# Moving the stages of a local transformer's feed-forward: moments, norm and all behind them one place on

## The chip, the cores and the metric

The kernel runs on one core of a Trainium2 chip. The core's engines work side by side, each through its own queue in program order: TensorE (PE, matmuls and transposes, writing to PSUM), VectorE (DVE), ScalarE (ACT), GpSimd (POOL) and SyncE (SP), whose queue issues the DMAs. The metric is the device time of one execution in microseconds (us), shown as the median of several runs.

## The reference

The model is four layers, each a cross-attention and a feed-forward of its own kind, over x of shape (4, 512, 128). The change is in the third layer's feed-forward, a small transformer of six layers with local attention (windows of 32) and a gated feed-forward. Cut to what matters:

```python
def ffn_layer(x, g, bln, W1, b1, W2, b2):
    mu = x.mean(-1, keepdims=True)
    var = ((x - mu) ** 2).mean(-1, keepdims=True)
    xn = (x - mu) / jnp.sqrt(var + 1e-05) * g + bln
    hg = xn @ W1 + b1                       # 128 -> 2 * 341
    a, gate = jnp.split(hg, 2, -1)
    return a * jax.nn.gelu(gate, approximate=False) @ W2 + b2   # 341 -> 128
for i in range(DEPTH):                      # 6
    x = attn_layer(shift_tokens(x), Wqkv[i], q_scale[i], k_scale[i], Wo[i]) + x
    x = ffn_layer(shift_tokens(x), ln_g[i], ln_b[i], W1[i], b1[i], W2[i], b2[i]) + x
```

attn_layer has 16 heads of 64: queries and keys are normalised to length 1, scaled and rotated, then each window of 32 attends to itself and the window before it.

## The kernel before

The four layers follow one another. All but the local transformer are scheduled by a small planner (class Plan). The local transformer (local_transformer, L1690) is written out by hand: a Python loop emits the instructions in the order in which each engine's queue will run them, and waits come only from data and buffers.

The state Y[b] holds one batch's 512 tokens, features on partitions. A tile is 128 tokens of one batch in one layer: 6 x 4 x 4 = 96 tiles. A row is one batch in one layer, that is 4 tiles: 24 rows. The loop at L2028 runs over periods n and is a software pipeline: period n works on three tiles at once, T = tiles[n] (products with the query, key and value weights, rotation), T1 = tiles[n-1] (transposes, scores, softmax) and T2 = tiles[n-2] (probabilities, averages, output projection, residual). Since the last tile of row m finishes its residual in period 4m + 5, the feed-forward of row m starts in period 4m + 6. Its phase in a period is (n - 6) % 4.

The order within one period, shortened, with the two or three places of the feed-forward:

- queries_or_keys(T, 0, 0), probabilities(T2), queries_or_keys(T, 0, 1), rotate(T, 0, 0)
- **place 0** of the feed-forward (L2053)
- average(T2, 0), turned(T1, 0), queries_or_keys(T, 1, 0), normalised(T2, 0), rotate(T, 0, 1), and the same with the second half
- attended(T2), for a batch's last tile swap (a copy of Y for the next row's values), scores(T1), the last rotations, normalise(T), softmax(T1), project_out(T2), residual(T2)
- **place 2** (L2090: the norm, in phase 0)
- values(T, 0), values(T, 1)
- **place 1** (L2095)

The feed-forward's pieces and their engines: four PE transposes of Y and a ScalarE copy to xn (L1951, L1953); moments, eight small DVE instructions and two of POOL (L510 to L515); the norm, four of DVE (L522); the turn, four PE transposes and one ScalarE instruction (L1962, L1964); ff_gate, PE products and ScalarE's gelu (L1973, L1976); ff_up, PE products and a DVE product with the gate (L1984, L1987); ff_down, six PE instructions and an addition to Y in two halves on DVE (L1996, L1711). Chunks 0 and 1 of the 341 hidden features are full (128), chunk 2 has 85. In the kernel before, four phases hold them:

| phase | place 0 | place 2 | place 1 |
|---|---|---|---|
| 0 | transposes, copy, moments | norm | |
| 1 | turn | | gate 0, 1 |
| 2 | gate 2 | | up 0, 1 |
| 3 | up 2 | | down |

Buffers that matter: PSUM has the pair "sc" (two banks, one buffer), which the feed-forward's transposes and products, and the scores of T1, all take in turn; the next user waits until the last has been read. "av" is another single pair, for averages and the output projection. "mm" has two buffers, for the query and key products; "tr" has two, for transposes and values. In SBUF the rotation's second term "rs" has two buffers and is freed by POOL's sum (L1797). Weights of a layer are loaded by load(i) in period 16(i - 1) + 7, into buffers of the layer before the last one; the scaled rotation tables of the next layer are made on POOL (L1755, L1761) in periods with n % 16 == 15.

Of the kernel before, what the change touches and what calls it, by code (L numbers as in the profile page):

```python
# [238 lines left out]
def tile_kernel(ctx: ExitStack, tc: tile.TileContext, A: dict, out: bass.AP):  # L239
# [129 lines left out]
    with banks(), tc.tile_pool(name="prep", bufs=1) as prep:  # L369
# [3 lines left out]
        rows = prep.tile([8, D], F32, name="rows0")  # L373
# [94 lines left out]
    def col(r):  # L468
        return cols[:, r : r + 1]
# [35 lines left out]
    def moments(src):  # L505

        st = small.tile([128, NT, 6], F32, name="ln_st")
        mv = small.tile([128, NT, 2], F32, name="ln_mv")
        for t in range(NT):
            V.bn_stats(st[:, t], src[:, t])  # L510
        for t in range(NT):
            V.bn_aggr(mv[:, t], st[:, t])
        rs = small.tile([128, NT], F32, name="ln_rs")
        G.tensor_scalar(rs, mv[:, :, 1], 1e-5, None, ALU.add)
        G.tensor_tensor(rs, rs, mhalf[:, :NT], ALU.pow)  # L515
        return mv, rs

    def layernorm(dst, src, found=None):

        mv, rs = found or moments(src)  # L520
        for t in range(NT):
            V.tensor_scalar(  # L522
                dst[:, t], src[:, t], mv[:, t, 0:1], rs[:, t : t + 1], ALU.subtract, ALU.mult
            )
# [1165 lines left out]
    def local_transformer(Y):  # L1690
        with ExitStack() as es:
# [8 lines left out]
            def pair(tag):  # L1700

                t = homes["pair"].tile([128, 2, 512], F32, tag=tag, bufs=1, name=f"ps_{tag}")
                return t

            def add_y(b, t, bias=None):
                for r, o in ((slice(0, 64), 0), (slice(64, 128), 1)):
                    dst = Y[b][r, o : o + S]
                    if bias is None:
                        V.tensor_tensor(dst, t[r], dst, ALU.add)
                    else:  # L1710
                        V.scalar_tensor_tensor(dst, t[r], bias[r], dst, ALU.add, ALU.add)  # L1711
# [189 lines left out]
            def probabilities(T):  # L1901
                T.PT = tp.tile([128, LH // 2, 128], F32, name="PT", bufs=1)
                for g in range(2):
                    SC.copy(T.PT[:, 4 * g : 4 * g + 4], to_features(T.P[:, 4 * g : 4 * g + 4]))
# [40 lines left out]
                    V.tensor_tensor(dst, t[r], dst, ALU.add)  # L1945


            def ff_moments(F):
                F.t = pair("sc")[:, 0].rearrange("p (a b) -> p a b", b=128)
                for tt in range(NT):  # L1950
                    PE.transpose(F.t[:, tt], Y[F.b][:, 128 * tt : 128 * tt + 128], ident)  # L1951
                F.xn = lnp.tile([128, NT, D], F32, name="xn")
                SC.copy(F.xn, F.t)  # L1953
                F.found = moments(F.xn)

            def ff_norm(F):
                layernorm(F.xn, F.xn, F.found)

            def ff_turn(F):
                t = pair("sc")[:, 0]  # L1960
                for tt in range(NT):
                    PE.transpose(t[:, 128 * tt : 128 * tt + 128], F.xn[:, tt], ident)  # L1962
                F.xnT = lnp.tile([128, S], F32, name="xnT")
                SC.activation(  # L1964
                    F.xnT, t, AF.Identity, scale=col(R_LG + F.i), bias=col(R_LB + F.i)
                )
                F.h = tp.tile([128, 3, S], F32, name="fh", bufs=1)

            def ff_gate(F, *chunks):
                t = pair("sc")  # L1970
                for j, c in enumerate(chunks):
                    n, o = CH_W[c], DI + 128 * c
                    PE.matmul(t[:n, j], F.w1[:, o : o + n], F.xnT, start=True, stop=True)  # L1973
                for j, c in enumerate(chunks):
                    n = CH_W[c]
                    SC.activation(  # L1976
                        F.h[:n, c], t[:n, j], AF.Gelu, bias=col(R_B1 + (3 + c) * DEPTH + F.i)[:n]
                    )

            def ff_up(F, *chunks):  # L1980
                t = pair("sc")
                for j, c in enumerate(chunks):
                    n, o = CH_W[c], 128 * c
                    PE.matmul(t[:n, j], F.w1[:, o : o + n], F.xnT, start=True, stop=True)  # L1984
                for j, c in enumerate(chunks):
                    n = CH_W[c]
                    V.scalar_tensor_tensor(  # L1987
                        F.h[:n, c], t[:n, j], col(R_B1 + c * DEPTH + F.i)[:n], F.h[:n, c],
                        ALU.add, ALU.mult,
                    )  # L1990

            def ff_down(F):
                t = pair("sc")[:, 0]
                for c in range(3):
                    n = CH_W[c]
                    PE.matmul(t, F.w2[:n, c], F.h[:n, c], start=(c == 0), stop=(c == 2))  # L1996
                add_y(F.b, t, col(R_B2 + F.i))
# [7 lines left out]
                )  # L2005
                swapped[b] = t

            def ff_stage(F, phase, second):
                F.w1, F.w2 = loaded[F.i][3:5]
                if phase == 0 and not second:  # L2010
                    ff_moments(F)
                elif phase == 1:
                    ff_gate(F, 0, 1) if second else ff_turn(F)
                elif phase == 2 and second:
                    ff_up(F, 0, 1)
                elif phase == 2:
                    ff_gate(F, 2)
                elif phase == 3:
                    ff_down(F) if second else ff_up(F, 2)

# [1 line left out]
            rows = [Tile(i, b, 0) for i in range(DEPTH) for b in range(B)]  # L2024
            loaded = {0: load(0)}
            tabs = {0: tables(loaded[0][5])}
            swap(0)
            for n in range(len(tiles) + 10):  # L2028
                T = tiles[n] if n < len(tiles) else None
                T1 = tiles[n - 1] if 0 <= n - 1 < len(tiles) else None  # L2030
                T2 = tiles[n - 2] if 0 <= n - 2 < len(tiles) else None
                m, phase = divmod(n - 6, 4)
                F = rows[m] if 0 <= m < len(rows) else None
                if T:
                    if n % 16 == 7 and T.i + 1 < DEPTH:
                        loaded[T.i + 1] = load(T.i + 1)
                    if n == 4:
                        fill, send, send_back = clear(lnp, 1)
                        fill(G)
                        send(DMA)  # L2040
                        send_back(DMA)
                    if n % 16 == 15 and T.i + 1 < DEPTH:
                        tabs[T.i + 1] = tables(loaded[T.i + 1][5])
                    T.before = tiles[n - 1] if T.tt else None
                    T.w, T.wv, T.wo = loaded[T.i][:3]
                    T.tabs = tabs[T.i]
                    queries_or_keys(T, 0, 0)
                if T2:
                    probabilities(T2)
                if T:  # L2050
                    queries_or_keys(T, 0, 1)
                    rotate(T, 0, 0)
                if F:  # L2053
                    ff_stage(F, phase, False)
                if T2:
                    average(T2, 0)
                if T1:
                    turned(T1, 0)
                if T:
                    queries_or_keys(T, 1, 0)  # L2060
                if T2:
                    normalised(T2, 0)
                if T:
                    rotate(T, 0, 1)
                if T2:
                    average(T2, 1)
                if T1:
                    turned(T1, 1)
                if T:
                    queries_or_keys(T, 1, 1)  # L2070
                if T2:
                    normalised(T2, 1)
                if T:
                    rotate(T, 1, 0)
                if T2:
                    attended(T2)
                if T and T.tt == NT - 1 and n + 1 < len(tiles):
                    swap(tiles[n + 1].b)
                if T1:
                    scores(T1)  # L2080
                if T:
                    rotate(T, 1, 1)
                if T:
                    normalise(T)
                if T1:
                    softmax(T1)
                if T2:
                    project_out(T2)
                    residual(T2)
                if F and phase == 0:  # L2090
                    ff_norm(F)
                if T:
                    values(T, 0)
                    values(T, 1)
                if F:  # L2095
                    ff_stage(F, phase, True)

            for b in range(B):
                for r, o in ((slice(0, 64), 0), (slice(64, 128), 1)):
# [39 lines left out]
```

## Time and profile before

| what | value |
|---|---|
| median of 5 runs | 2558.78 us |
| lowest, highest | 2552.48, 2562.35 us |
| profiled execution | 2560.74 us |
| its span, first to last instruction | 2559.0 us |
| mean granted clock of TensorE | 0.944 |
| PE, DVE, ACT, POOL busy | 2290.8, 1789.6, 1243.1, 1540.0 us |
| first and last row maximum of the loop (L1893) | 579.9 and 2222.3 us |
| first and last instruction of the feed-forward's moments (L510) | 655.1 and 2242.1 us |

A line of the timeline gives start and duration in us, the engine, the source line, the operation, the tile written and those read with their shapes, and how many instructions of this kind stand together; behind it in brackets the idle time of that engine just before and what ended it. A line of the groups gives the count, the busy time in us, the mean in ns of one instruction, and the idle time before these instructions with what ended most of it. A busy PE is not PE at its peak: matmuls are pipelined and their ends are modelled.

### The profile page before, as it was taken

To read this page: it belongs to the slowest core of one execution; us is meant where nothing else is said; L and a number is where in the kernel's file an instruction comes from. 1 tells how busy PE (TensorE), PEld (TensorE's weight loads), DVE (VectorE), ACT (ScalarE), POOL (GpSimd) and SP (SyncE) were. 2 spreads that over 40 slices of the span, in tenths; PEclk is the share of its full clock that TensorE was granted. 3 is DMA by queue.
4 is the path that set the end of the run, shared out by engine and by line. 5 is a ranking of instruction groups with operands and counts; after the bars stand their busy time and mean duration, and the time that the engine had idled before them with its cause. 6 is when DMAs were issued, how large, how long until landed. Compare 5 with 4: busy or idle time off the path is not lost.

```text
span 2559.0 us, 87683 instructions
## 1 busy us (share of the span) xinstructions
PE 2290.8 (90%) x37341; PEld 1487.5 (58%) x37341; DVE 1789.6 (70%) x4016; ACT 1243.1 (49%) x2185; POOL 1540.0 (60%) x2613
## 2 busy tenths in 40 slices
PE   7968869968899999999999999999999999878676
PEld 3537624446666666666666666666666666634364
DVE  5533375758787888888888888788888888655422
ACT  3522225535555555555555555555555555423232
POOL 2332311348778777777777777877777777532333
PEclk9959969979999999999999999999999999978688
DMA  6210110014511112111211121111211111111022
GB/s 164 76 31 28 33 46 2 1 47 83 127 34 31 29 47 61 27 34 34 68 34 34 30 75 34 27 33 41 64 30 34 33 27 34 28 48 37 19 72 82
DMA packets 134305, 116.21 MB, mean 45 GB/s; under 512 B 29505, under 2 KB 102700, under 8 KB 133916
## 3 DMA queue, kind: packets, MB, share of 16 engines
q1 hardware_dynamic: 128373, 102.81, 15.4%
q0 software_dynamic: 4608, 7.35, 0.9%
q8 instruction: 296, 4.85, 0.8%
q14 instruction: 93, 0.76, 0.1%
q10 hardware_dynamic: 935, 0.43, 0.1%
HBM read 42.84 MB, written 21.52 MB: 25 GB/s over the span
## 4 chain that ended last, share of the span: by engine, by line
PE 57%; DVE 21%; issue 7%; POOL 5%; ACT 5%; DMA 3%; SPq 1%; another core or an unknown queue 1%; POOLq 0%; ACTq 0%; DVEq 0%
PE ps_tr L582 8%; PE ps_mm L1774 8%; PE ps_av L1938 4%; PE ps_av L1914 4%; PE ps_tr L1853 3%; DVE rc L1784 3%; DVE rs L1787 3%; DVE ss L1796 3%; PE ps_sc L1883 3%; PE ps_sc L1984 3%; PE ps_sc L1996 3%; PE ps L773 2%; PE ps L1312 2%; DVE P L1894 2%; PE ps L782 2%
## 5 line engine op out<-in xcount | busy, mean ns | idle before, releaser
L1797 POOL TENSOR_TENSOR rc<-rc,rs 128x512 f32<-128x512 f32 x384 | 488.2, 1274 | 232.4 <-DVE rs L1787 186.1
L1774 PE MATMUL ps_mm<-wqk,y 128*128 128x512 f32 x768 | 396.9, 599 | 10.6 <-DVE rs L1787 7.4
L1818 POOL TENSOR_TENSOR rc<-rc,rn_y 128x512 f32<-128x512 f32 x384 | 388.3, 1042 | 7.5
L1784 DVE TENSOR_TENSOR rc<-ps_mm,tabs 128x512 f32<-128x512 f32 x384 | 262.0, 682 | 159.4 <-ACT sq L1776 144.4
L1899 ACT ACTIVATE P<-P 128x1024 f32<-128x1024 f32 x96 | 101.5, 1057 | 424.1 <-DVE P L1894 424.1
L1776 ACT ACTIVATE sq<-ps_mm 128x512 f32<-128x512 f32 x384 | 230.7, 601 | 151.4 <-PE ps_mm L1774 103.0
L1787 DVE TENSOR_TENSOR rs<-ps_mm,tabs 128x512 f32<-128x512 f32 x384 | 261.1, 680 | 5.6 <-POOL rc L1797 5.5
L1796 DVE TENSOR_REDUCE ss<-sq 128x8 f32<-128x512 f32 x384 | 259.1, 675 | 0.0
L582 PE MATMUL ps_tr<-cst,rc 128*128 128x128 f32 x1536 | 210.5, 280 | 6.0 <-POOL rc L1818 4.4
L1914 PEld LDWEIGHTS ps_av<-v,PT 64*32 64x32 f32 x12288 | 137.4, 105 | 126.0 <-PE ps_tr L582 54.9
L1938 PE MATMUL ps_av<-aT,wo 128*128 128x128 f32 x1536 | 200.2, 283 | 4.8 <-issue 4.5
L1938 PEld LDWEIGHTS ps_av<-aT,wo 128*128 128x128 f32 x1536 | 180.6, 192 | 15.1 <-issue 6.6
L582 PEld LDWEIGHTS ps_tr<-cst,rc 128*128 128x128 f32 x1536 | 165.2, 141 | 25.8 <-POOL rc L1818 5.5
L1883 PE MATMUL ps_sc<-kT,qT 64*32 64x64 f32 x12288 | 147.2, 225 | 34.3 <-issue 27.1
L1914 PE MATMUL ps_av<-v,PT 64*32 64x65 f32 x12288 | 168.3, 225 | 6.0 <-DVE attn L1924 5.7
L1017 POOL DMA_INDIRECT back<-ye,to x80 | 77.7, 971 | 158.0 <-DVE ye L1131 113.1
L1883 PEld LDWEIGHTS ps_sc<-kT,qT 64*32 64x32 f32 x12288 | 140.5, 105 | 45.1 <-issue 31.0
L1774 PEld LDWEIGHTS ps_mm<-wqk,y 128*128 128x128 f32 x768 | 124.6, 192 | 60.9 <-issue 45.5
L763 ACT ACTIVATE P<-ps,deltaT 77x512 f32<-77x512 f32 x192 | 115.3, 682 | 82.2 <-PE ps L757 70.7
L1830 ACT COPY kT<-ps_tr 128x512 f32<-128x512 f32 x192 | 103.1, 589 | 81.5 <-PE ps_tr L582 81.5
L1830 ACT COPY qT<-ps_tr 128x512 f32<-128x512 f32 x192 | 103.2, 589 | 75.4 <-PE ps_tr L582 72.8
L1924 DVE TENSOR_TENSOR attn<-ps_av,la_den 128x512 f32<-128x512 f32 x192 | 132.7, 691 | 6.6
(392 smaller groups left out, 4502.2 us busy)
## 6 DMA issues: line engine op xcount, KB each, us to landing
v<-v SPq DMA_DIRECT2D x432, 65.0 KB
v<-v SPq DMA_DIRECT2D x96, 195.0 KB
wqk<-in_L_ffn_Wqkv_dram SPq DMA_DIRECT2D x24, 256.0 KB
sent<-xn SPq DMA_DIRECT2D x2, 2210.0 KB
xe<-sent SPq DMA_DIRECT2D x16, 260.0 KB
back<-xn SPq DMA_DIRECT2D x2, 2048.0 KB
raw<-in_L_ffn_W_dram SPq DMA_DIRECT2D x8, 512.0 KB
yb<-back SPq DMA_DIRECT2D x16, 256.0 KB
```

The costliest lines, as they stand in the source:

```text
L582: PE.transpose(t[:, i], src[:, i], ident)
L1774: PE.matmul(t, lhs, T.w[2 * kind + c], start=True, stop=True)
L1776: SC.activation(sq, t, AF.Square)
L1784: V.tensor_tensor(a, t, bc(T.tabs[:, 2 * kind, tt], [128, 8, LD], 1), ALU.mult)
L1787: V.tensor_tensor(r.rearrange("p h (x d) -> p h x d", x=2), t.rearrange("p h (x d) -> p h x d", x=2)[:, :, ::-1], bc(T.tabs[:, 2 * kind + ...
L1796: V.tensor_reduce(T.ss[:, kind, 8 * c : 8 * c + 8], sq, AX.X, ALU.add)
L1797: G.tensor_tensor(a, a, r, ALU.add)
L1818: G.tensor_tensor(a, a, bc(y[:, o : o + 8], [128, 8, LD], 2), ALU.mult)
L1830: SC.copy(t[:, 4 * c : 4 * c + 4, lead:], to_features(T.rot[kind, c].rearrange("p (k x) d -> p k (x d)", x=2)),)
L1883: PE.matmul(T.banks[32 * w : 32 * w + 32, z, k], T.qT[r, k, 32 * w : 32 * w + 32], T.kT[r, k, 32 * w : 32 * w + 64], start=False, stop=Tru ...
L1914: PE.matmul(T.means[32 * w : 32 * w + 32, x0, k], T.PT[r, 4 * g + k, 32 * w : 32 * w + 32], (T.v1 if w % 2 else T.v2)[r, x0, 4 * g + k], s ...
L1938: PE.matmul(t, T.wo[:, c], T.aT[:, c], start=(c == 0), stop=(c == 7))
```

## The change

The feed-forward of a row is spread over five periods; the fifth is at the same time the first of the next row. Transposes and copy stay where they were. Moments go from place 0 to place 2 of phase 0, the norm from place 2 of phase 0 to place 2 of phase 1, and everything behind it one period on. Up 2 and down of row m - 1 now stand in phase 0 of row m, up 2 just ahead of row m's transposes at place 0, and down at place 1.

| phase | place 0 | place 2 | place 1 |
|---|---|---|---|
| 0 | up 2 of the last row, transposes, copy | moments | down of the last row |
| 1 | | norm | |
| 2 | turn | | gate 0, 1 |
| 3 | gate 2 | | up 0, 1 |

The instructions, their shapes and their number stay the same.

```diff
-            def ff_moments(F):
+            def ff_tokens(F):
                 F.t = pair("sc")[:, 0].rearrange("p (a b) -> p a b", b=128)
                 for tt in range(NT):
                     PE.transpose(F.t[:, tt], Y[F.b][:, 128 * tt : 128 * tt + 128], ident)
                 F.xn = lnp.tile([128, NT, D], F32, name="xn")
                 SC.copy(F.xn, F.t)
-                F.found = moments(F.xn)
...
-            def ff_stage(F, phase, second):
-                F.w1, F.w2 = loaded[F.i][3:5]
-                if phase == 0 and not second:
-                    ff_moments(F)
-                elif phase == 1:
-                    ff_gate(F, 0, 1) if second else ff_turn(F)
-                elif phase == 2 and second:
+            def row(m):
+                F = rows[m] if 0 <= m < len(rows) else None
+                if F:
+                    F.w1, F.w2 = loaded[F.i][3:5]
+                return F
+
+            def ff_stage(m, phase, place):
+                F, last = row(m), row(m - 1)
+                if last and phase == 0 and place == 0:
+                    ff_up(last, 2)
+                if last and phase == 0 and place == 1:
+                    ff_down(last)
+                at = 3 * phase + place
+                if F and at == 0:
+                    ff_tokens(F)
+                elif F and at == 2:
+                    F.found = moments(F.xn)
+                elif F and at == 5:
+                    ff_norm(F)
+                elif F and at == 6:
+                    ff_turn(F)
+                elif F and at == 7:
+                    ff_gate(F, 0, 1)
+                elif F and at == 9:
+                    ff_gate(F, 2)
+                elif F and at == 10:
                     ff_up(F, 0, 1)
-                elif phase == 2:
-                    ff_gate(F, 2)
-                elif phase == 3:
-                    ff_down(F) if second else ff_up(F, 2)
...
-                if F:
-                    ff_stage(F, phase, False)
+                ff_stage(m, phase, 0)
...
-                if F and phase == 0:
-                    ff_norm(F)
+                ff_stage(m, phase, 2)
                 if T:
                     values(T, 0)
                     values(T, 1)
-                if F:
-                    ff_stage(F, phase, True)
+                ff_stage(m, phase, 1)
```

More of the change, by code (lines that the diff above doesn't have):

```diff
@@ L2032, in local_transformer @@
                 m, phase = divmod(n - 6, 4)
-                F = rows[m] if 0 <= m < len(rows) else None
                 if T:
```

## The prediction

> **What bounds the kernel now.** I read the page first, then the idle times by line inside the loop, then the timeline of VectorE (DVE) over one row of the feed-forward.
>
> ```profile
> PE 2290.8 (90%) x37341; PEld 1487.5 (58%) x37341; DVE 1789.6 (70%) x4016; ACT 1243.1 (49%) x2185; POOL 1540.0 (60%) x2613
> ...
> L1784 DVE TENSOR_TENSOR rc<-ps_mm,tabs 128x512 f32<-128x512 f32 x384 | 262.0, 682 | 159.4 <-ACT sq L1776 144.4
> ```
>
> The loop is so tight that TensorE (PE) looks like the bound. The timeline says more. I call the start of the row maximum (L1893) the mark of a period, the stretch from a mark to the next period's first rotation product (L1784) the head, and the rest up to the next mark the tail. Quarter p is the period whose phase is p; its interval ends at its mark. Lines of quarters 3 and 0 (and the marks round them):
>
> ```profile
> 1305.00 1.22 DVE L1893 TENSOR_REDUCE la_mx<-ps_sc 128x16 f32<-128x1024 f32 x1
> ...
> 1312.62 0.69 DVE L1784 TENSOR_TENSOR rc<-ps_mm,tabs 128x512 f32<-128x512 f32 x1 [4.65 <-ACT sq L1776]
> ...
> 1322.53 1.22 DVE L1893 TENSOR_REDUCE la_mx<-ps_sc 128x16 f32<-128x1024 f32 x1
> ...
> 1327.14 1.41 DVE L1987 SCALAR_TENSOR_TENSOR fh<-ps_sc,cols,fh 128x512 f32<-128x512 f32 x2 [1.64 <-PE ps_sc L1984]
> 1328.69 0.69 DVE L1784 TENSOR_TENSOR rc<-ps_mm,tabs 128x512 f32<-128x512 f32 x1
> ...
> 1330.60 0.75 DVE L1987 SCALAR_TENSOR_TENSOR fh<-ps_sc,cols,fh 85x512 f32<-85x512 f32 x1
> 1331.39 0.21 DVE L1923 RECIPROCAL la_den<-ps_av 128x8 f32<-128x8 f32 x1
> ...
> 1339.59 1.22 DVE L1893 TENSOR_REDUCE la_mx<-ps_sc 128x16 f32<-128x1024 f32 x1
> ...
> 1347.06 0.69 DVE L1784 TENSOR_TENSOR rc<-ps_mm,tabs 128x512 f32<-128x512 f32 x1
> ...
> 1350.34 0.18 DVE L1923 RECIPROCAL la_den<-ps_av 128x8 f32<-128x8 f32 x1
> ...
> 1358.43 1.22 DVE L1893 TENSOR_REDUCE la_mx<-ps_sc 128x16 f32<-128x1024 f32 x1
> ```
>
> What to see: in every tail DVE runs end to end. Quarter 2, whose tail holds no feed-forward work for DVE, takes 9.91 us (1312.62 to 1322.53). Quarter 3 takes 10.90: the third ff_up product (0.75) is in it. Quarter 0 takes 11.37: the moments and a wait for their input are in it. Quarter 1 takes 10.57 (1294.43 to 1305.00). The heads are 7.62 in quarter 2 (table load and gelus on ScalarE), 6.16 in quarter 3, 7.03 to 7.47 in quarter 0 (down, then its addition on DVE), 5.05 in quarter 1. So a microsecond that DVE is blocked in a tail is a microsecond of the interval; one in a head with a gap is free. The gaps, between 650 and 2200 us:
>
> ```profile
> L1711 DVE SCALAR_TENSOR_TENSOR y<-ps_sc,cols,y 64x512 f32<-64x512 f32 x44 | 33.1, 751 | 62.2 <-PE ps_sc L1996 61.9
> ...
> L510 DVE BATCH_NORM_STATS2 ln_st<-xn 128x6 f32<-128x128 f32 x92 | 20.1, 281 | 7.6 <-ACT xn L1953 7.6
> ```
>
> **The change, part by part.** The work per row stays the same; only places move. Quarter by quarter:
>
> *Moments leave the tail of quarter 0* for the head of quarter 1, behind residual and ahead of down's addition. Today that head waits for down 61.9 / 22 = 2.8 us per row with DVE idle; four bn_stats and four bn_aggr take 0.88 + 0.36 = 1.2 us and fit. If down came sooner the 1.2 would show. The tail loses what lies above quarter 2's 9.91: 11.37 - 9.91 = 1.46. Not all: without the moments DVE reaches the reciprocal 1.85 after L1784, and PE ends the averaging it reads at about 1.8 to 1.9, so I leave 0.1: **-1.35**. Bounds -1.46 and -1.15 (the busy time alone).
>
> *Tokens get a wait.* In quarter 0 PE now issues the third ff_up product and directly after it the four token transposes. Both write the one "sc" pair, so the transposes wait until DVE has read the product. DVE's queue holds the three instructions of the first rotation ahead of that read. In old quarter 3 this read starts at 1330.60 just as PE ends the product (L1984, 1329.54 + 1.02) and ends at 1331.35. Release to PE takes 0.14 (attn ends 1351.24, the averaging L1914 starts 1351.38). Then 0.53 for the transposes (L1951 at 1347.90, next matmul 1348.43), 0.1 more as nothing was prefetched, 0.86 averaging, 0.05 to the reciprocal: 1333.03 instead of 1331.39, **+1.60**. Behind the waiting transposes on PE stand both averagings, all further transposes, products and scores; DVE waits at the reciprocal in a tail, so nothing absorbs it. Bounds: +0.5, if the wait were hidden and only the transposes counted (the turn's transposes cost quarter 1 about that: its reciprocal waits 0.43); +2.2, with transposes at the 1.15 of the cold ones at 2244.63 and the 0.33 that L510 waits.
>
> The xn copy on ScalarE keeps its place ahead of the queries' copy, which came 0.7 later anyway: nothing. Net per row +1.60 - 1.35 = **+0.25**, between -0.96 and +1.05; 22 rows in the loop: **+5.5**.
>
> *Norm* goes to the head of quarter 2, *turn* to its place 0. Both stand to each other and to the attention work as they did one quarter earlier (5.05 + 10.57 = 15.62 today). *Gates* move to 2/3, *first ups* to the end of 3: heads 7.62 and 6.16 unchanged: 0. What differs is the tile index under them: POOL's clearing of v2 (two of 0.53 us) now falls in the gate's period, where DVE's first rotation is late and POOL waited 0.7 and more for it: 0. Swap on ScalarE stays with its tile, and the gates leave its neighbourhood: 0. SP's queue is passed by nothing: no DMA moves in it, and the weights that load(i+1) overwrites are released one period before it issues instead of two; its issues come some 8 us after that: 0.
>
> *POOL* gets the two instructions of the moments (0.23 + 1.04) ahead of the v1 memset and the first sum L1797 of quarter 1. That sum then ends 4.0 us after L1784; it is needed by the "rs" buffer's reuse at 5.9: 0. Once per layer (five times) the tables (3.06) stand there too: today they cost 16.88 - 15.62 = 1.26 in quarter 1. With quarter 1's head 2.0 longer and 1.35 more on POOL some 0.3 is saved each: **-1.5**, bounds -6.3 and +6.5 (all hidden; or the 1.3 fully added).
>
> *Row 0* has no row ahead: no wait, but the moments go: **-1.4**.
>
> *The end* lies open, as nothing covers it. Period 96 loses table load and gelus (1.28 + 1.26) and gets the turn (0.6): -1.9. Then the last row queues behind both ups of row 22 rather than down: up 1.9, product on DVE 1.5, up 1.2, DVE 0.8, release 0.1 after project_out's end at 2235.95 put the tokens at 2241.5 (today 2240.23); down of row 22 and its addition (2.74 + 1.51) now stand ahead of the last norm on DVE, which starts near 2247.1 instead of 2244.14: +3.0. Together **+1.1**, bounds -2 and +5.
>
> Sum: 5.5 - 1.5 - 1.4 + 1.1 = **+3.7 us**. The profiled execution took 2560.74 (span 2559.0), 2 above the median of 2558.78, so it would become 2564.4, and the median **2562.5**.
>
> One rule against the change, in sentences of its own. In the loop the granted clock is 1.00 (1200 to 1270 us); in the last row, after an idle 3.77 us, it is 0.50 (2244 to 2248), and four gate instructions take 3.53 us instead of 1.98. The Trainium skill, "TensorE: Matmul & The Clock Gate", section "HAM oscillation — how this bites in real kernels", says that PE gaps longer than about 3.4 us bring the half clock back. The new wait is 0.85 us, so by the rule the loop keeps its clock, as in the sum; were one such wait enough, a window of 3.4 us at half speed would add up to 1.7 us to each row, an estimate of 37 us in all. Row and rule agree on the place where it matters, the last row.
>
> **Rivals.**
> *Slower, by the wait on "sc".* If the transposes' wait costs over 1.8 us per row instead of 1.6 (DVE's read later, or the PE delay spilling from the tail of quarter 0 into values and down of quarter 1), the sum passes +7.7. At the upper bound of 2.2 it is +17: 2576. For it: DVE and PE reach the product at the same moment, so any lag of DVE goes to PE in full. Against: scores end over 1 us ahead of the mark.
> *Slower, moments uncovered.* If down no longer holds DVE for 2.8 us, 22 x 1.2 = 27 us come back: 2590. Against: quarter 1's PE order up to down is today's of quarter 0.
> *Faster.* PE stalls on issue in the scores of every second row (1.12 us at 1200.77, 0.55 at 1338.87), and intervals of quarter 0 are then 0.5 to 0.7 longer. If the new idle time lets PE's instructions run ahead, 11 x 0.6 = 7 go; with the wait at 1.4 another 4: about -8, 2551.
> *Nothing changes*, since the bound is PE's work (which is the same): +0, 2559. Against: the tails are DVE's.
>
> **How the numbers follow.** Two results closer than 0.3% (7.7 us) can't be told apart. The worked case and "nothing" lie within: 0.50. The two slower rivals: 0.28 and 0.07, together 0.35. The faster one: 0.15. The likeliest case's own range is 2553 to 2570 (net per row -0.2 to +0.6). The range given, 2551 to 2577, takes in the faster rival's end and the first slower one and leaves out the bounds at which several uncertain terms meet.
>
> **What would show it.** Right: quarter 0's tail 12.3 to 12.6 with PE waiting about 0.9 at L1951's transposes for L1987; quarter 1's head 7.0 to 7.5 with bn_stats in it and its tail near 10.0; quarters 2 and 3 at 15.6 and 17.5. Wrong: reciprocals in quarter 0 that don't wait; L1711's idle falling below its 2.8 minus 1.2; L1787 waiting for POOL in more than the table rows; marks of quarter 2 or 3 off today's 15.62 and 17.53.

## The result, and the profile after

The changed kernel takes 2565.96 us (median of 35 runs) against 2556.35 us for the kernel before (61 runs, more than were shown at first). The ratio is 1.0035, with a 95% interval of 1.0025 to 1.0044: slower by about 9 us. The profiled execution has a span of 2568.0 us, 9.0 above that of before. The time lies in the range given (2551 to 2577). The forecast's most likely case was a change too small to tell, with a centre of +3.7 us; what came is on the slow side, just past the 0.3% line that the text drew, where the forecast had put its slower rivals.

The page of the kernel after, as shown of before:

```profile
PE 2298.8 (90%) x37341; PEld 1485.4 (58%) x37341; DVE 1795.7 (70%) x4016; ACT 1243.4 (48%) x2183; POOL 1537.6 (60%) x2613
...
L1784 DVE TENSOR_TENSOR rc<-ps_mm,tabs 128x512 f32<-128x512 f32 x384 | 262.0, 682 | 162.2 <-ACT sq L1776 146.7
```

Nothing moves there by more than 9 us, and the number of instructions is the same on PE, DVE and POOL (ScalarE has two table loads fewer, one beside a gelu and one beside an exponential); the page can't tell a loss of 9 from two large terms of opposite sign. The timeline of DVE can. These lines are one quarter 0 (first rotation product at 1280.08, mark at 1292.45) and the quarter 1 behind it (mark at 1310.30). L1986 is the product of ff_up, which was L1987 before; L1951, L1784, L1893 and L1923 kept their numbers:

```profile
1280.08 0.69 DVE L1784 TENSOR_TENSOR rc<-ps_mm,tabs 128x512 f32<-128x512 f32 x1
...
1281.98 0.75 DVE L1986 SCALAR_TENSOR_TENSOR fh<-ps_sc,cols,fh 85x512 f32<-85x512 f32 x1
1284.27 0.21 DVE L1923 RECIPROCAL la_den<-ps_av 128x8 f32<-128x8 f32 x1 [1.54 <-PE ps_av L1914]
...
1292.45 1.22 DVE L1893 TENSOR_REDUCE la_mx<-ps_sc 128x16 f32<-128x1024 f32 x1
...
1295.46 0.87 DVE L510 BATCH_NORM_STATS2 ln_st<-xn 128x6 f32<-128x128 f32 x4
1296.26 0.36 DVE L512 BATCH_NORM_AGGREGATE ln_mv<-ln_st 128x2 f32<-128x6 f32 x4
1298.68 1.52 DVE L1711 SCALAR_TENSOR_TENSOR y<-ps_sc,cols,y 64x512 f32<-64x512 f32 x2 [2.06 <-PE ps_sc L1995]
1300.23 0.69 DVE L1784 TENSOR_TENSOR rc<-ps_mm,tabs 128x512 f32<-128x512 f32 x1
...
1302.07 0.21 DVE L1923 RECIPROCAL la_den<-ps_av 128x8 f32<-128x8 f32 x1
...
1310.30 1.22 DVE L1893 TENSOR_REDUCE la_mx<-ps_sc 128x16 f32<-128x1024 f32 x1
```

Two things are to be seen. In quarter 0 DVE now stands still for 1.54 us before the reciprocal, in a tail where nothing takes the time back; this tail is 12.37 us long. In the head of quarter 1 the moments (0.87 and 0.36) lie in a stretch in which DVE still waits 2.06 for down: they cost nothing there. What holds DVE is on PE, in the same quarter 0:

```profile
1280.92 1.02 PE L1983 MATMUL ps_sc<-xnT,lw 128*85 128x512 f32 x2
1282.78 0.66 PE L1951 MATMUL ps_sc<-cst,y 128*128 128x128 f32 x4 [0.84 <-DVE fh L1986]
1283.37 0.86 PE L1914 MATMUL ps_av<-v,PT 64*32 64x65 f32 x64
```

PE ends the third up product, and then the token transposes wait 0.84 us for DVE to read that product out of "sc". In old quarter 3 of the kernel before, the averaging followed that product at once:

```profile
1329.54 1.02 PE L1984 MATMUL ps_sc<-xnT,lw 128*85 128x512 f32 x2
1330.49 0.86 PE L1914 MATMUL ps_av<-v,PT 64*32 64x65 f32 x64
```

PE's waits between 750 and 2200 us (total, times, longest) and then DVE's groups between 650 and 2200 us show it for all rows:

```profile
PE ps_sc L1951 <- DVE fh L1986: 17.7, 21, 0.8
```

```profile
L1711 DVE SCALAR_TENSOR_TENSOR y<-ps_sc,cols,y 64x512 f32<-64x512 f32 x42 | 31.6, 751 | 34.5 <-PE ps_sc L1995 34.2
...
L510 DVE BATCH_NORM_STATS2 ln_st<-xn 128x6 f32<-128x128 f32 x88 | 19.2, 281 | 0.7
```

The idle time ahead of down's addition fell from 2.8 to 34.2 / 21 = 1.6 us per row: the moments took 1.2 of it.

From the starts of L1893 and L1784 in the two timelines, mean of the 21 rows between periods 11 and 94, in us. Old and new quarters are put side by side by the work that they hold:

| new quarter (what it holds) | head + tail before | head + tail after | difference |
|---|---|---|---|
| 0 (up 0, 1 in the head; up 2; now the transposes too), was 3 | 6.26 + 10.93 | 6.37 + 12.44 | +1.62 |
| 1 (down; its tail without transposes and moments), was 0 | 7.35 + 11.36 | 7.34 + 10.44 | -0.94 |
| 2 (norm, turn), was 1 | 5.06 + 10.89 | 5.08 + 10.59 | -0.29 |
| 3 (gates), was 2 | 7.62 + 9.94 | 7.62 + 9.92 | -0.02 |
| a row | 69.43 | 69.80 | +0.37 |

The -0.29 and 0.27 of the 10.44 are the rotation tables, whose cost went from the third line to the second. From the mark of period 11 to that of period 95 the loop takes 1458.0 us before and 1465.4 after: +7.4.

### The profile page after: what moved, and what is told of

It reads as the page before. It is cut to its first block, busy times and chain, and to the rows that moved or that the text cites. A ratio compares the mean times of both kernels' runs of the same rounds, so it can differ in the third digit from the quotient of the medians.

```text
span 2568.0 us, 87685 instructions
## 1 busy us (share of the span) xinstructions
PE 2298.8 (90%) x37341; PEld 1485.4 (58%) x37341; DVE 1795.7 (70%) x4016; ACT 1243.4 (48%) x2183; POOL 1537.6 (60%) x2613
## 3 DMA queue, kind: packets, MB, share of 16 engines
q0 software_dynamic: 4608, 7.35, 0.9%
## 4 chain that ended last, share of the span: by engine, by line
PE 63%; DVE 19%; issue 6%; ACT 5%; POOL 4%; DMA 2%; SPq 1%; another core or an unknown queue 1%; ACTq 0%; POOLq 0%; DVEq 0%
PE ps_tr L582 10%; PE ps_mm L1774 9%; PE ps_av L1938 5%; PE ps_av L1914 5%; PE ps_tr L1853 4%; PE ps_sc L1883 3%; DVE rc L1784 3%; DVE rs L1787 3%; DVE ss L1796 3%; PE ps_sc L1995 3%; PE ps L773 2%; PE ps_sc L1983 2%; PE ps L782 2%; PE ps L1312 2%; PE ps L757 2%
## 5 line engine op out<-in xcount | busy, mean ns | idle before, releaser
L1784 DVE TENSOR_TENSOR rc<-ps_mm,tabs 128x512 f32<-128x512 f32 x384 | 262.0, 682 | 162.2 <-ACT sq L1776 146.7
```

The source lines that it names most:

```text
L1784: V.tensor_tensor(a, t, bc(T.tabs[:, 2 * kind, tt], [128, 8, LD], 1), ALU.mult)
```

## The experiments

The theory: two large terms nearly cancel. The transposes behind the third up product, with their wait for the "sc" pair, cost 1.6 us per row, the moments' way out of a full tail gives back 1.2 to 1.35, and the rest moves without cost. The rivals: the loss is POOL's (two more instructions ahead of quarter 1's sums), or belongs to the longer pipeline as such, or one of the two terms is not there. The chips of these runs differ in speed from the first one and from each other (2507.76 us for the kernel before in the first four, 2562.18 in the last three), so only ratios to the kernel before on the same chip are compared, and lengths inside the loop.

### Token transposes in a buffer of their own

```diff
             def ff_tokens(F):
-                F.t = pair("sc")[:, 0].rearrange("p (a b) -> p a b", b=128)
+                F.t = p_tr(128, NT, 128)
```

> The changed kernel, with the four token transposes written to one of the two 'tr' buffers instead of the pair 'sc' that up 2 of the row ahead has just taken. Theory (the loss is the transposes' wait for DVE's read of that product): the wait goes, the reciprocal of quarter 0 comes 3.3 us after the first rotation product instead of 4.2, quarter 0's tail falls from 12.44 to about 11.5, 22 times 0.93 = 20 us, and about 1 at the end: some 12 us below the kernel before, ratio 0.995. Rival (the loss sits elsewhere: two more POOL instructions ahead of quarter 1's sums, or the longer pipeline): ratio stays at 1.003 to 1.004.

Ratio 0.9916 (0.9899 to 0.9934). Quarter 0's mean tail is 11.41, its reciprocal comes 3.21 after the first product, and the loop from mark 11 to mark 95 takes 1441.3 us, 24.1 less than the changed kernel and 16.7 less than the kernel before. DVE in one quarter 0:

```profile
1243.45 0.74 DVE L1986 SCALAR_TENSOR_TENSOR fh<-ps_sc,cols,fh 85x512 f32<-85x512 f32 x1
1244.76 0.21 DVE L1923 RECIPROCAL la_den<-ps_av 128x8 f32<-128x8 f32 x1 [0.56 <-PE ps_av L1914]
```

and PE beside it:

```profile
1242.39 1.02 PE L1983 MATMUL ps_sc<-xnT,lw 128*85 128x512 f32 x2
1243.25 0.60 PE L1951 MATMUL ps_tr<-cst,y 128*128 128x128 f32 x4
1243.78 0.86 PE L1914 MATMUL ps_av<-v,PT 64*32 64x65 f32 x64
```

The transposes follow the product without a gap, and of DVE's 1.54 there is 0.56 left: the transposes' own time. The wait is the cause of the loss, and removing it beats both kernels. The ratio fell below the 0.995 expected. In the loop that shows: 16.7 us below the kernel before, where 21 x 0.93 - 7.4 would be 12, as the interval of quarter 0 gave 1.08 and that of quarter 1 another 0.12 per row. The other 4 of some 21 us lie outside these marks, where one profile of each does not settle them.

### The same edit in the kernel before

> The kernel before with the same edit. There no product stands right ahead of the token transposes, so by the theory nothing waits that could be released: ratio 1.000, within 0.001, and quarter 0's tail stays at 11.36. Rival (the 'sc' pair is short in general, or 'tr' is simply the better buffer): 0.995 or less.

Ratio 0.9986 (0.9975 to 0.9996): a gain of about 3 us, a little more than allowed for, and clear of the rival's 0.995. The loop does not have it: 1457.6 us between the marks against 1458.0 (the two profiles are of different chips; that they agree is what lets lengths in the loop be compared), quarter 0's tail 11.37 against 11.36. So in the loop "tr" is no better in itself; the buffer matters where two users of "sc" follow each other. Where the 3 us come from stays open: in the last row the transposes start 1.9 us earlier, since they no longer wait for down's addition, but in this profile the rest of that row took longer (see the last section).

### Tokens first, then up 2

```diff
-                if last and phase == 0 and place == 0:
-                    ff_up(last, 2)
...
                 if F and at == 0:
                     ff_tokens(F)
...
                 elif F and at == 10:
                     ff_up(F, 0, 1)
+                if last and phase == 0 and place == 0:
+                    ff_up(last, 2)
```

> The changed kernel with the order at place 0 of quarter 0 turned round: token transposes first, then up 2 of the row ahead. Theory (what costs is two users of the one pair back to back, in either order): now up 2 waits for ScalarE's copy of the tokens, its DVE product is late, the reciprocal comes again about 4.2 us after the first rotation product: ratio 1.002 to 1.004. Rival (it is DVE's late read of the product alone that holds PE, so the order decides): tail of quarter 0 about 11.5 and ratio 0.995.

Ratio 1.0032 (1.0015 to 1.0049), quarter 0's tail 12.38, the reciprocal 4.17 after the first product: as the changed kernel. Now ScalarE's copy holds PE. PE's waits between 750 and 2200 us, then DVE:

```profile
PE ps_sc L1983 <- ACT xn L1953: 16.5, 21, 0.8
```

```profile
1244.02 0.75 DVE L1986 SCALAR_TENSOR_TENSOR fh<-ps_sc,cols,fh 85x512 f32<-85x512 f32 x1 [1.48 <-PE ps_sc L1983]
1244.81 0.21 DVE L1923 RECIPROCAL la_den<-ps_av 128x8 f32<-128x8 f32 x1
```

The order does not matter; two users of a single buffer back to back do. The same 1.5 us of DVE's standstill sits one instruction earlier.

### Moments back in quarter 0

```diff
                 if F and at == 0:
                     ff_tokens(F)
-                elif F and at == 2:
                     F.found = moments(F.xn)
```

> The changed kernel with the moments back at place 0 of quarter 0, right behind the token copy; all else stays on five periods. Theory (the moments' move from a full tail into a head with a gap gains 1.2 to 1.35 us per row): quarter 0's tail rises by 1.2 to 1.46 to about 13.8, quarter 1 stays within 0.1: 23 times 1.3 = 30 us above the changed kernel, ratio to the kernel before about 1.015. Rival (the moments are hidden by the new wait on PE anyway): ratio stays at 1.003 to 1.005.

Ratio 1.0065 (1.0040 to 1.0090). The theory's 1.015 is out. The interval still reaches into the rival's 1.003 to 1.005, but the tail decides: the moments' place does matter, by half of what the theory said. Quarter 0's tail went from 12.44 to 13.18, by 0.74 and not by 1.2 to 1.46. And quarter 1 changed where it was expected not to: its tail is 10.08 instead of 10.44, with no table row above 10.17, and its head is 0.11 shorter. So the loop takes 1471.3 us, only 5.9 above the changed kernel. DVE in quarter 0:

```profile
1256.28 0.75 DVE L1986 SCALAR_TENSOR_TENSOR fh<-ps_sc,cols,fh 85x512 f32<-85x512 f32 x1
1258.39 0.87 DVE L510 BATCH_NORM_STATS2 ln_st<-xn 128x6 f32<-128x128 f32 x4 [1.37 <-ACT xn L1953]
1259.18 0.36 DVE L512 BATCH_NORM_AGGREGATE ln_mv<-ln_st 128x2 f32<-128x6 f32 x4
1259.46 0.18 DVE L1923 RECIPROCAL la_den<-ps_av 128x8 f32<-128x8 f32 x1
```

The moments run while PE averages, so part of them lies in the time that DVE would spend waiting for the reciprocal's input.

### Own buffer, moments back

Both edits (token transposes in "tr", moments at place 0).

> The changed kernel with the token transposes in a 'tr' buffer, and the moments back at place 0 of quarter 0. Theory (with the wait on 'sc' gone, the moments in the tail cost their full length again, where with it they partly lay in the time that DVE waited anyway): quarter 0's tail rises from 11.4 to 12.6, by 1.2 instead of 0.74; the tables are free in quarter 1 (5.6 us less), so 22 times 1.2 less 5.6 = 21 us above the buffer alone, ratio about 1.000. Rival (moments in this tail cost 0.74 whatever stands beside them): 0.995 to 0.996.

Ratio 0.9954 (0.9935 to 0.9973): the rival's number, and the theory's 1.000 is outside. Quarter 0's tail is 12.12 against 11.41 with the buffer alone: 0.71. So the moments cost about 0.7 in this tail with or without the wait on "sc". The likely reason is in these lines:

```profile
1284.48 0.75 DVE L1986 SCALAR_TENSOR_TENSOR fh<-ps_sc,cols,fh 85x512 f32<-85x512 f32 x1
1285.54 0.87 DVE L510 BATCH_NORM_STATS2 ln_st<-xn 128x6 f32<-128x128 f32 x4 [0.31 <-ACT xn L1953]
```

Even without the wait on "sc" (and with the moments elsewhere, as in the first experiment), DVE has a gap of 0.56 before the reciprocal there, because PE has the transposes to do between the product and the averaging; the moments fill it. A cost read from one tail (1.46 in old quarter 0) does not hold in another with a different gap.

### Tables one period earlier

```diff
-                    if n % 16 == 15 and T.i + 1 < DEPTH:
+                    if n % 16 == 14 and T.i + 1 < DEPTH:
                         tabs[T.i + 1] = tables(loaded[T.i + 1][5])
```

> The changed kernel with only the tables one period earlier. Theory (in quarter 1 the moments' two POOL instructions and the tables stand together ahead of the first sum, so the longer head gave no cover): quarter 1's tail 10.1 in the table rows instead of 11.2, ratio 1.001 to 1.002. Rival (it is the buffer wait alone that decides): 1.0035.

Ratio 1.0014 (0.9989 to 1.0038): the expected value, but the interval holds the rival's too. The loop's length decides better: 1460.1 us, 5.3 less than the changed kernel, and quarter 1's mean tail 10.17 instead of 10.44; in the table rows it is 10.1 to 10.2 in four of five (10.9 once) instead of 11.2 in all. What cost the time in the changed kernel, on POOL in a table row and then on DVE:

```profile
812.74 1.04 POOL L515 TENSOR_TENSOR ln_rs<-ln_rs,mhalf 128x4 f32<-128x4 f32 x1
813.73 0.13 POOL L1847 MEMSET v<- 128x16 f32 x1
813.80 0.73 POOL L1755 TENSOR_TENSOR tabs<-cst,qs 128x256 f32<-128x256 f32 x1
...
816.82 2.51 POOL L1797 TENSOR_TENSOR rc<-rc,rs 128x512 f32<-128x512 f32 x2
```

```profile
818.13 0.69 DVE L1787 TENSOR_TENSOR rs<-ps_mm,tabs 128x512 f32<-128x512 f32 x1 [0.91 <-POOL rc L1797]
```

The moments' POOL instructions, the tables and only then the first sum: DVE waits 0.91 for its "rs" buffer.

### Own buffer and tables earlier

Both edits together.

> The changed kernel with the token transposes in a 'tr' buffer and the next layer's rotation tables made one period earlier (in quarter 0 instead of quarter 1). Theory: quarter 1's tail loses its 11.2 in the five table rows (10.1 in all), 5 times 1.1 = 5.6 us, on top of what the buffer alone gives (ratio 0.9916): 0.989 to 0.990. Rival (POOL's 3.06 us cost the same wherever they stand): 0.9916 as with the buffer alone, with quarter 0's tail up by 1 in five rows.

Ratio 0.9900 (0.9877 to 0.9922), as expected, but the interval overlaps that of the buffer alone, and the loop does not bear it out: 1441.1 us against 1441.3 in the two profiles. Quarter 1's mean tail is 0.17 shorter (10.21 against 10.38), while the rest of the row together is as much longer, with single rows out of line by half a microsecond. That the tables' move adds to the buffer's gain is not shown. This is the fastest ratio measured, about 1% below the kernel before.

## Why the prediction was right or wrong

**Moments leave the tail (-1.35 per row).** The mechanism is right: they are hidden in the head of quarter 1, with 1.6 us of idle left. The size was a little too large. With the table rows' share taken out (10.44 - 5 x 1.12 / 21) quarter 1's tail is 10.17, against 11.36: -1.19. The usual row has 10.10, since PE's second averaging now ends 0.1 behind DVE; a few rows have 10.6. The term holds against the old tail only: put back into the new one, the same moments cost 0.74, so this term and the next do not simply add.

**Tokens get a wait (+1.60).** Right in place, and nearly in size: 0.84 us of PE's wait in 21 of 21 rows, DVE idle for 1.54, the tail 1.51 longer. The working itself comes to 1.64 (1333.03 - 1331.39), not to 1.60; the reciprocal comes 4.22 us after the first rotation product instead of 2.70, so 1.52 later. Release took 0.05 (1282.73 to 1282.78) and not 0.14, and the transposes 0.06 more than unhindered (0.66 against 0.60) and not 0.1. The interval's +1.62 has another 0.11 from the head, which the forecast did not have, so its nearness to 1.60 is partly luck. The first experiment shows the cause: without the wait the interval is 1.08 shorter, and the transposes' own time is what stays.

**Norm, turn, gates, first ups (0).** Right: 15.67 against 15.65 when the table rows' share is taken out (15.95 - 5 x 1.27 / 21), and 17.55 against 17.56. The clearing of v2 under another quarter cost nothing.

**Tables (-1.5 in all).** Too hopeful. Five rows cost 11.22 - 10.10 = 1.12 each instead of 1.27: -0.75. The estimate of 0.3 saved per row was the step that failed; 0.15 was left of the longer head. With the tables one period earlier most of the 1.12 goes: those rows have 10.30 in the mean.

**Row 0 (-1.4).** Not confirmed. The first six periods with feed-forward work take 102.5 us before and 102.8 after, but this stretch takes 99.7 to 104.0 in the other profiles of the changed kernel's relatives, and the fifth mark, up to which the code is the same, already comes 2.7 us later in the second profile. One profile of each can't settle a term of this size.

**The end (+1.1).** Near: period 96 lost 2.55 (15.32 to 12.77; -1.9 forecast), and from its mark to the first addition to x it takes 47.43 instead of 44.03, +3.40 (+3.0 forecast): +0.85. As worked, the last norm now waits for down's addition. DVE of the kernel after:

```profile
2253.86 1.51 DVE L1711 SCALAR_TENSOR_TENSOR y<-ps_sc,cols,y 64x512 f32<-64x512 f32 x2 [1.75 <-PE ps_sc L1995]
2255.41 1.11 DVE L522 TENSOR_SCALAR xn<-xn,ln_mv,ln_rs 128x128 f32<-128x128 f32 x4
```

**The sum.** From mark 11 to mark 95 the working gives 21 x 0.25 - 1.5 = +3.8; the profiles give +7.4. The missing 3.6 is the moments' 0.16 per row (3.4) with the tables' 0.75, less some noise. With +0.3 for the first six periods and +0.85 for the end that makes +8.6, and the runs gave +9. So near an agreement is partly luck, for stretches with the same code differ too between the two profiles: by +2.7 us up to the fifth mark, by -2.2 behind the first addition to x. A net of two terms of 35 and 26 us (22 rows of 1.60 and 1.19) was bound to be soft: an error of a tenth in one of them is as large as the net that was forecast.

**The rivals.** The slower one ("sc" above 1.8 per row) did not come by its mechanism, though the total lies where it had put it: the term was 1.62, and the excess over the forecast came mostly from the moments and the tables. "Moments uncovered" is out, by 1.6 us of idle left. "Nothing changes" is out, the ratio's interval excludes 1. The faster one, PE's instructions running ahead in the new idle time, left no trace in PE's stalls on issue in the scores between 750 and 2200 us, the first line before, the second after:

```profile
PE ps_sc L1883 <- issue: 19.0, 20, 1.5
```

```profile
PE ps_sc L1883 <- issue: 20.0, 21, 1.6
```

**The clock rule.** In the loop after the change the granted clock is 1.00 (750 to 2200 us), with a wait of 0.84 us in every row: as the Trainium skill has it for gaps below about 3.4 us ("TensorE: Matmul & The Clock Gate", section "HAM oscillation — how this bites in real kernels"). The 37 us of the other reading did not come. In the last row the measurement differs from that rule: after the change PE's longest idle time between the mark of period 96 and the last row's gates is 2.08 us, and the granted clock still falls, from 1.00 (2226.00 to 2257.60 us) to 0.50 (2257.70 to 2261.00). The four gate instructions take 1.96 us for row 22 and 3.58 for the last one. PE, kernel after:

```profile
2232.89 1.96 PE L1972 MATMUL ps_sc<-xnT,lw 128*128 128x512 f32 x4 [0.76 <-DVE P L1894]
...
2255.90 1.00 PE L1961 MATMUL ps_sc<-cst,xn 128*128 128x128 f32 x4 [2.08 <-DVE xn L522]
2257.78 3.58 PE L1972 MATMUL ps_sc<-xnT,lw 128*128 128x512 f32 x4 [0.87 <-ACT xnT L1963]
```

## What to carry to other kernels

When a stage is moved in a hand-ordered pipeline, look at what will stand next to it on the same single buffer: two users back to back cost the whole chain read, release and restart (here 1.5 us of a full tail for a wait of 0.84), in either order, and a second buffer that happens to be free at that place is the cheap cure (it took 1.1 us per row off; the transposes' own 0.56 stayed). Read the price of moving an instruction from the gap at the new place and the gap that is left at the old one: the same moments were worth 1.2 us in one tail and 0.7 in another. And when two large terms nearly cancel, give the direction little weight, or find the edit that keeps only one of them.

## What the runs showed of the hardware that was not expected

In the last row, where little work is left for PE, an earlier start did not bring an earlier end. In the kernel before, the last of the last norm's four instructions starts 22.56 us after the mark of period 96, and the addition to x comes 21.5 us after it; with the token transposes in "tr" it starts 21.16 after the mark, and the addition comes 24.1 us after it. The granted clock over that stretch is 0.72 in the one profile and 0.55 in the other, and two products of 85 features, 1.09 us before, take 2.00. The first line is of the kernel before, the second of the kernel before with the edit (stretch, busy times with counts, then the granted clock, DMA share and GB/s):

```profile
2244.60:2266.40 21.80, 15.09 (x30) 5.50 (x30) 4.32 (x9) 4.01 (x5) 1.24 (x7) 0.72 0.02 5
```

```profile
2217.20:2241.60 24.40, 17.70 (x30) 5.84 (x30) 4.34 (x8) 4.01 (x5) 1.20 (x6) 0.55 0.02 3
```

PE's busy time differs by 2.6 us there (15.09 against 17.70), as much as the stretch. The other profiles say that this is no single case: in the five kernels with the token transposes in "sc" the stretch from that norm instruction to the addition takes 21.1 to 21.5 us at a granted clock of 0.73 to 0.76, in the four with "tr" 22.1 to 24.1 us at 0.55 to 0.69, on both chips that ran both kinds. So the lower clock goes with the edit; why it does is not shown.
